# Half of the first layer's output turned by a DRAM trip and VectorE's square transposes, half by TensorE, with the three written-out orders replaced

## Chip, cores and metric

The kernel runs on one core of one Trainium2 chip, on real inputs, and is judged by the device time of that core in microseconds (us), lower being better. All arithmetic that matters is f32.

## What is computed

64 independent graphs of 256 nodes each pass through two attention layers; `x` is 64 x 256 x 512, `adj` 64 x 256 x 256.

```python
h = relu(layernorm(x))
# layer 0: two attention products in a row, mask = adj or self
xl = (h @ W1)            # 512 -> 4 heads x 256
z  = elu(concat_heads(softmax(mask(leaky_relu(a_src + a_dst))).T @ xl) + b1)   # 256 x 1024
xl = (z @ W2)            # 1024 -> 512, one head
x  = x + softmax(...).T @ xl + b2
# layer 1: eight heads of 64
h  = relu(layernorm(x))
xp = h @ W_proj          # 512 -> 512
x  = x + relu(softmax(mask(leaky_relu(...))) @ xp)
```

The change concerns `z`, the first attention's output: 256 nodes by 1024 features, the features of heads 0 and 1 in columns 0 to 511. It must be turned (features on partitions) before TensorE can multiply it with `W2`.

## The kernel before, in words

The program is one straight list of instructions, without loops on the chip. A `Graph` object has one method for each step of a graph's work, and three strings, `head`, `order` and `tail`, write out by hand the order in which the steps of neighbouring graphs are emitted: `0 gat1 1 0` in round `r` is step `gat1` with arguments 1, 0 of graph `r + 0`, and `-1 m3 p5` a step of graph `r - 1`. `head` runs once, `order` for r = 1 to 63, `tail` once. So three graphs are always in flight, and every engine works through its own instructions in the order of the strings: an instruction that waits holds up all that its engine has after it. SyncE (SP) issues nearly all DMAs and is such a queue too.

The steps that are named later, for one graph:

- `load`, `masks`, `stats1`, `norm1`: input, adjacency masks (VectorE), layer statistics (VectorE, then a power on GpSimd), normalisation (ScalarE, L189).
- `away1`, `turn1`: the normalised `h` is written to DRAM (`kept_h`, L203), read back with its 32-column squares on other partitions (L204), and turned by VectorE's 32 x 32 transposes (`back`, L209).
- `m1a`, `m1b`, `m2`, `m3`: the products with W1 (two halves), W2 and W_proj. Each is done with 7 block products, `p1` to `p7` (L54), over sums of the turned operand that `left` makes on GpSimd (L215 to L218). `p1` reads block 0 of the turned operand, `p2` block 1, `p5` block 3 (the first of GpSimd's sums), `p6` block 2 (the second). `p1`, `p6` and `p7` each copy their PSUM sum by ScalarE (`kept`, L60); `p2`, `p3` and `c22` add on VectorE (L260).
- `exp1`/`rows1`/`edges1`/`gat1`/`out1`/`elu1`: the first attention. `rows` sends the exponentials through DRAM to broadcast them (L239, L244), `edges1 h` makes the weights of head h (ScalarE L289, VectorE L290), `gat1 g t` is the product of heads 2g and 2g+1 for half t of the nodes (TensorE L394), `out1 g t` normalises (VectorE L402, L404) and makes exp(-relu(-z)) on ScalarE (L407, L408), `elu1 g t` ends it on VectorE (L413).
- `turn2 r k`: 4 of TensorE's transposes (L196) into a PSUM tile, and ScalarE's copy to the operand `h1s` of `m2` (L422). Four such steps turn the 16 blocks of `z`.
- `edges2`/`gat2`/`out2`, `stats3`/`norm3`/`turn3`, `edges3`/`gat3`/`out3`/`store`: second attention (TensorE L448, VectorE L455, L458), second normalisation, turned by TensorE with ScalarE's copy (L196, L229), third attention (L500, L506, L508) and output. `cap3` issues DMA transposes of the mask.

PSUM tiles `pm` have four buffers, `sum` two, the transposes' tiles `pt` two. `z` has one buffer for each half of the nodes, `h1s` one.

Of the kernel before, what the change touches and what calls it, by code (L numbers as in the profile page):

```python
# [17 lines left out]
P = 128  # L18
# [79 lines left out]
def short_path(ctx, tc, flags, x, adj, w1, att_src1, att_dst1, b1, w2, att_src2, att_dst2, b2, w_proj, w_att,  # L98
               b_att, out):

    nc = tc.nc
    B, N, D = x.shape
    H1, F1 = att_src1.shape
    HF = H1 * F1
# [23 lines left out]
    ident = const.tile([P, P], F32, name="ident")  # L128
# [21 lines left out]
    w2_sb = const.tile([P, 7, HC // 2, L2 + Q], F32, name="w2_sb")  # L150
# [42 lines left out]
    def turn(h, c, pt):  # L193
        for k in range(2):
            for t in range(T):
                nc.tensor.transpose(pt[:, k, t * P:(t + 1) * P], h(t, c + k), ident)  # L196
# [95 lines left out]
    class Graph:  # L292
# [120 lines left out]
            nc.vector.scalar_tensor_tensor(z, self.e["ez", g, t], -1.0, z, ALU.add, ALU.max)  # L413
# [12 lines left out]

        def exp2(self):
# [138 lines left out]
    class Weights:  # L566
# [49 lines left out]


    head = """
        0 turn0, w dots1 0, 0 masks, 0 m1b p1, w dots1 2, w dots1 5, w sums1 1, w dots1 1, 0 m1b p6, w dots1
        3, 0 bias, 0 m1b p2, 0 m1b p7, w dots2 0, 0 m1b p5, w dots1 4, w dots1 6, w dots1 7, 0 m1a p1, w  # L620
        sums1 0, 0 m1b c22, 0 m1b p4, 0 m1a p6, w dots2 3, 0 m1a p7, 0 m1a p5, w dots2 2, w dots2 7, w dots2
        5, 0 m1a p2, 0 m1a c22, w dots2 1, 0 m1a p3, w dots2 6, 0 m1a p4, w dots2 4, w columns2, 0 m1b p3, w
        sums2 0, w sums2 1, 0 exp1, 0 rows1, w sums2 2, 0 caps, w sums2 3, 0 edges1 1, 0 edges1 0, 0 edges1
        3, 0 cap3, 0 edges1 2, 0 gat1 0 0, 0 out1 0 0, 0 gat1 0 1, 0 out1 0 1, 0 gat1 1 0, 0 elu1 0 0, 0
        out1 1 0, 0 elu1 0 1, w load3, 0 gat1 1 1, 1 load, 0 out1 1 1, w dots3 7, 1 stats1, 0 turn2 0 0, 0
        elu1 1 0, 1 masks, 0 turn2 0 1, 0 elu1 1 1, 1 norm1, w dots3 1, 0 m2 p1, w dots3 2, w dots3 0, w
        dots3 6, 1 away1, 0 turn2 1 0, 0 turn2 1 1, w dots3 5, w dots3 4, w dots3 3, 1 turn1, 0 m2 p6, w
        sums3 0, 0 m2 p2, w sums3 1, w sums3 2, 0 m2 p7, 0 m2 p4, 0 m2 p5, 1 m1a p1, 1 m1a p6, 0 m2 c22, 1
        m1a p5, 0 m2 p3, 0 exp2, 0 rows2, 1 m1a p7, 1 m1a c22, 1 m1b p1, w sums3 3, 1 m1a p4, 1 m1a p3, 1
        m1a p2, 1 exp1, 1 rows1, 1 bias, 1 m1b p6, 1 m1b p2, 1 m1b p5, 1 caps  # L630
    """
# [13 lines left out]
    tail = """
        -2 range, 0 m1b p5, 0 m1a p2, -1 edges2, -2 gat3 0 0, 0 m1a c22, 0 m1b p6, -2 gat3 0 1, -2 out3 0 1,
        0 m1b p2, -2 edges3 5, -1 gat2 0, 0 exp1, 0 rows1, 0 m1a p4, -1 out2 0, -1 stats3 0, -2 edges3 7, -1
        gat2 1, -2 gat3 1 0, -1 out2 1, -1 stats3 1, -1 norm3, -2 out3 0 0, -2 gat3 1 1, -2 out3 1 1, -1
        turn3, -1 m3 p1, -1 m3 p2, -1 m3 p5, -1 m3 p6, -1 m3 p7, -1 m3 c22, -2 out3 1 0, -1 m3 p4, -1 m3 p3,
        -1 exp3, -1 rows3, -1 range, -1 edges3 1, -1 edges3 4, -1 edges3 0, -1 edges3 3, -1 edges3 2, -1  # L650
        edges3 5, -1 edges3 7, -1 edges3 6, -1 gat3 0 0, -1 gat3 0 1, -2 store, -1 gat3 1 1, -1 out3 0 1, -1
        out3 1 1, -1 gat3 1 0, -1 out3 0 0, -1 out3 1 0, -1 store
    """
# [295 lines left out]
```

## Time and profile before

| what | value |
|---|---|
| median of 3 runs | 3218.17 us (3216.63 to 3219.29) |
| profiled execution | 3218.9 us, its span 3217.2 us |
| granted TensorE clock, mean | 0.993 |
| TensorE (PE) busy | 3133.7 us, 97% of the span |
| weight loads (PEld) busy | 2670.7 us, 83% |
| VectorE (DVE) busy | 2282.5 us, 71% |
| ScalarE (ACT) busy | 1917.4 us, 60% |
| GpSimd (POOL) busy | 1179.1 us, 37% |
| SP's queue of DMAs | 31.9% of 16 DMA engines |

Times in the profile are microseconds unless marked ns. A line of groups gives the code line, engine, operation, output <- inputs, shape and count, then busy time and the mean ns of one instruction, then the engine's idle time before them and what ended it. A line of the timeline gives start, length, engine, line and count of merged instructions. Matmuls overlap each other, so the step from one start to the next, and not the length of one, is what a matmul costs the engine.

### The profile page before, as it was taken

How to read it: one execution, taken by the hardware profiler on the slowest of the kernel's cores; microseconds unless marked ns; L12 is line 12 of the kernel's file. 1: busy time of each engine (PE TensorE's matmuls, PEld its weight loads, DVE VectorE, ACT ScalarE, POOL GpSimd, SP SyncE). 2: the span in 40 equal slices, each digit the busy share in tenths (PEclk: the TensorE clock that was granted, in tenths of full speed). 3: DMA queues.
4: the chain of work that ended last, by engine and by line, in shares of the span. 5: the costliest groups of instructions: out<-in, count | busy, mean ns of one | idle time of the engine just before them, and what ended most of it. 6: DMA issues, size and time to landing. Idle time of an engine off the chain costs nothing. (4 is left out here: it accounts for less than half of the span.)

```text
span 3217.2 us, 60904 instructions
## 1 busy us (share of the span) xinstructions
PE 3133.7 (97%) x21808; PEld 2670.7 (83%) x21808; DVE 2282.5 (71%) x6379; ACT 1917.4 (60%) x4867; POOL 1179.1 (37%) x1434
## 2 busy tenths in 40 slices
PE   4999999999999999999999999999999999999997
PEld 3788888888888888888888888888888888888886
DVE  7667677677677677676676776776776776776765
ACT  2456566656666665665565566566666666655654
POOL 2343343333433433433433433434434334334332
PEclk8999999999999999999999999999999999999999
DMA  4233333333333333333333333332333333333331
GB/s 143 57 95 83 89 88 91 83 91 87 89 87 92 88 86 84 96 81 90 97 80 90 88 89 83 91 92 83 92 87 88 88 91 88 81 89 96 81 90 35
DMA packets 439842, 281.49 MB, mean 87 GB/s; under 512 B 109168, under 2 KB 389744, under 8 KB 439536
## 3 DMA queue, kind: packets, MB, share of 16 engines
q1 hardware_dynamic: 438160, 275.43, 31.9%
q8 instruction: 177, 2.90, 0.4%
q10 hardware_dynamic: 1376, 2.10, 0.2%
q14 instruction: 129, 1.06, 0.1%
HBM read 199.36 MB, written 69.70 MB: 84 GB/s over the span
## 5 line engine op out<-in xcount | busy, mean ns | idle before, releaser
L289 ACT ACTIVATE wy<-bc,exs_sb 128x256 f32<-128x256 f32 x1646 | 706.9, 498 | 176.1 <-DMA bc<-kept 129.3
L260 DVE TENSOR_TENSOR xl<-pm,kept 128x256 f32<-128x256 f32 (+2 forms) x768 | 321.5, 419 | 285.8 <-PE pm L54 208.7
L510 POOL TENSOR_TENSOR x<-x,o 128x256 f32<-128x256 f32 x256 | 181.1, 728 | 916.0 <-DVE r L506 884.4
L394 PE MATMUL pm<-xl,e 128*128 128x257 f32 x2048 | 489.9, 386 | 17.6 <-DVE e L290 13.6
L290 DVE SCALAR_TENSOR_TENSOR e<-wy,exs_sb,cap 128x256 f32<-128x256 f32 x1024 | 435.8, 478 | 92.4 <-ACT wy L289 92.4
L54 PE MATMUL sum<-w_sb,h1s 128*128 128x257 f32 x2048 | 489.0, 381 | 9.3 <-POOL h1s L216 7.0
L60 ACT ACTIVATE kept<-sum 128x264 f32<-128x264 f32 (+3 forms) x768 | 276.5, 376 | 341.9 <-PE sum L54 336.6
L54 PEld LDWEIGHTS sum<-w_sb,h1s 128*128 128x128 f32 x2048 | 389.3, 190 | 68.7 <-POOL h1s L216 7.2
L394 PEld LDWEIGHTS pm<-xl,e 128*128 128x128 f32 x2048 | 374.3, 190 | 84.0 <-DVE e L290 14.9
L54 PE MATMUL pm<-w_sb,h1s 128*128 128x257 f32 x1536 | 371.1, 383 | 10.4 <-DVE xl L260 6.5
L54 PEld LDWEIGHTS pm<-w_sb,h1s 128*128 128x128 f32 x1536 | 287.0, 190 | 74.9 <-POOL hs L216 20.1
L181 POOL TENSOR_TENSOR rstd<-ve,neg_half 128x2 f32<-128x2 f32 x128 | 117.6, 919 | 630.3 <-DVE ve L179 630.3
L500 PEld LDWEIGHTS pm<-xl,e 128*64 128x64 f32 x8192 | 251.0, 138 | 45.4 <-DVE e L290 23.4
L54 PE MATMUL sum<-w1a_sb,hs 128*128 128x260 f32 x1024 | 269.6, 386 | 11.7 <-ACT kept L60 4.5
L290 DVE SCALAR_TENSOR_TENSOR e<-wy,exs_sb,mask 128x256 f32<-128x256 f32 x640 | 270.3, 480 | 13.1 <-ACT wy L289 12.8
L54 PE MATMUL sum<-w1b_sb,hs 128*128 128x256 f32 x1024 | 271.9, 388 | 2.9 <-ACT hs L353 1.5
L500 PE MATMUL pm<-xl,e 128*64 128x65 f32 x8192 | 270.1, 224 | 2.1 <-DVE e L290 1.3
L54 PE MATMUL sum<-wp_sb,hs 128*128 128x264 f32 x1024 | 270.8, 387 | 1.3 <-ACT kept L60 1.1
L407 ACT ACTIVATE ez<-z 128x512 f32<-128x512 f32 x256 | 159.6, 623 | 178.5 <-DVE z L404 178.5
L404 DVE SCALAR_TENSOR_TENSOR z<-pm,r,b_sb 128x256 f32<-128x256 f32 x512 | 247.8, 484 | 18.3
L448 PE MATMUL pm<-xl,e 128*128 128x257 f32 (+1 forms) x1024 | 242.9, 380 | 1.1 <-DVE e L290 1.1
L54 PEld LDWEIGHTS sum<-w1a_sb,hs 128*128 128x128 f32 x1024 | 191.4, 190 | 50.2 <-issue 15.2
(99 smaller groups left out, 5013.4 us busy)
## 6 DMA issues: line engine op xcount, KB each, us to landing
bc<-kept SPq DMA_DIRECT2D x380, 256.0 KB, 5.7
xs<-in_x_dram SPq DMA_DIRECT2D x64, 512.0 KB, 3.9
out_dram<-x SPq DMA_DIRECT2D x64, 512.0 KB, 2.8
kept_h<-h SPq DMA_DIRECT2D x63, 512.0 KB, 3.2
h<-kept_h SPq DMA_DIRECT2D x63, 512.0 KB, 3.7
ad<-in_adj_dram SPq DMA_DIRECT2D x64, 256.0 KB, 4.3
bc<-kept SPq DMA_DIRECT2D x63, 128.0 KB, 4.8
kept<-wt SPq DMA_DIRECT2D x190, 16.0 KB, 1.4
```

The costliest lines, as they stand in the source:

```text
L54: self.nc.tensor.matmul(to[:, :self.n], self.lhs[:, i, c, :], self.rhs[:, i, c, :], start=(first and c == 0), stop=(last and c == self.nk ...
L60: self.nc.scalar.activation(s[:, :self.n], self.sum[:, :self.n], AF.Copy)
L181: nc.gpsimd.tensor_tensor(rstd, ve[:, 0, :], neg_half, ALU.pow)
L260: nc.vector.tensor_tensor(dst, pm, add, ALU.add)
L289: nc.scalar.activation(wy.rearrange("p (t j i) -> p t j i", t=T, j=4), bc, AF.Copy, scale=yw)
L290: nc.vector.scalar_tensor_tensor(dst, wy, xw, mask, ALU.max, op)
L394: nc.tensor.matmul(pm[:, :Q + 1], self.e[1, h][:, s, t * P:(t + 1) * P], xl1[:, s, h, L1:], start=(s == 0), stop=(s == T - 1))
L404: nc.vector.scalar_tensor_tensor(z[:, sl], pm[:, :Q], r, b1_sb[:, sl], ALU.mult, ALU.add)
L407: nc.scalar.activation(ez, z[:, 2 * g * F1:2 * (g + 1) * F1], AF.Relu, scale=-1.0)
L448: nc.tensor.matmul(pm[:, :n], self.e[2][:, s, t * P:(t + 1) * P], xl2[:, s, half, L2:L2 + n], start=(s == 0), stop=(s == T - 1))
L500: nc.tensor.matmul(pv[q:q + 64, h, :], self.e[3, a * G + h][:, s, t * P + q:t * P + q + 64], xl3[:, s, a * G + h, :], start=(s == 0), stop ...
L510: nc.gpsimd.tensor_tensor(to, to, o.rearrange("p h k -> p (h k)"), ALU.add)
```

## The change

Heads 0 and 1 of `z` (the first 512 columns) leave TensorE's transposes, for every graph but the first and the last. `send2 t`, after `elu1 0 t`, writes these columns of one half of the nodes to DRAM and reads them back into the same place with the 32-column squares redistributed; `back2 t` turns them by one transpose of VectorE straight into `h1s`. For the first and the last graph `back2` uses TensorE and ScalarE as before. `turn2 k` remains for heads 2 and 3. Since the new path leaves the features of heads 0 and 1 in another order, the first 512 rows of W2 are loaded in that order. The strings `head`, `order` and `tail` are written anew: `head` now reaches into round 2, `order` runs for r = 2 to 62, and `tail` takes more of the last rounds.

```diff
-        def turn2(self, r, k):
-            if r == 0 and k == 0:
+        def send2(self, t):
+            if t == 0:
                 self.a2 = work.tile([P, 7, HC // 2, P], F32, name="h1s", bufs=1)
                 self.m2 = Product(nc, ps_sum, ps_mm, work, self.a2, w2_sb, put2)
+            if 0 < self.b < B - 1:
+                z = self.zt[t][:, :HF // 2]
+                kept = dram.tile([4, P, P], F32, name="kept_z")
+                nc.sync.dma_start(kept.rearrange("a p e -> p a e"), z.rearrange("p (a e) -> p a e", a=4))
+                nc.sync.dma_start(z, kept.rearrange("a (j q) e -> (a j) (q e)", q=4))
+
+        def back2(self, t):
+            z, a = self.zt[t][:, :HF // 2], self.a2[:, 4 * t]
+            if 0 < self.b < B - 1:
+                nc.vector.transpose(a.rearrange("p k (j q) -> p q k j", q=4), z.rearrange("p (q i c) -> p q c i", q=4, c=4))
+            else:
+                pt = ps_tr.tile([P, 2, N], F32, name="pt")
+                for k in range(HC // 2):
+                    nc.tensor.transpose(pt[:, k // 2, k % 2 * P:(k % 2 + 1) * P], z.rearrange("p (m k) -> p k m", k=4)[:, k],
+                                        ident)
+                nc.scalar.activation(a.rearrange("p k q -> p (k q)"), pt.rearrange("p k q -> p (k q)"), AF.Copy)
+
+        def turn2(self, k):
             pt = ps_tr.tile([P, 2, N], F32, name="pt")
-            turn(lambda t, c: self.zt[t][:, c * P:(c + 1) * P], 4 * r + 2 * k, pt)
-            nc.scalar.activation(self.a2[:, r:r + 5:4, 2 * k:2 * k + 2], pt.rearrange("p k (t q) -> p t k q", t=T),
-                                 AF.Copy)
-            if r == 1 and k == 1:
+            turn(lambda t, c: self.zt[t][:, c * P:(c + 1) * P], 4 + 2 * k, pt)
+            nc.scalar.activation(self.a2[:, 1:6:4, 2 * k:2 * k + 2], pt.rearrange("p k (t q) -> p t k q", t=T), AF.Copy)
+            if k == 1:
                 left(self.a2, HC // 2)
...
-    bring(w2_sb, w2, 0, 0, (nc.sync, nc.sync))
+    for half in range(2):
+        nc.sync.dma_start(blocks(w2_sb)[0][half][:, :, -Q:],
+                          w2[:HF // 2, half * Q:(half + 1) * Q].rearrange("(p c) f -> p c f", p=P))
...
     order = """
-        -2 edges3 7, -2 gat3 0 0, -2 edges3 5, -2 gat3 0 1, -1 edges2, 0 m1b p7, -2 out3 0 1, -2 out3 0 0,
-        -1 gat2 0, 0 m1b c22, -1 out2 0, -1 stats3 0, 0 m1b p3, -1 gat2 1, 0 edges1 0, 0 edges1 1, 0 m1b p4,
-        -1 out2 1, 0 cap3, 1 load, 0 gat1 0 0, 0 edges1 2, 0 edges1 3, 0 out1 0 0, -2 gat3 1 1, -2 gat3 1 0,
-        -1 stats3 1, 0 gat1 0 1, -1 norm3, -2 out3 1 1, -2 out3 1 0, -2 store, 0 out1 0 1, 0 elu1 0 0, 0
-        elu1 0 1, 0 gat1 1 0, -1 turn3, 0 out1 1 0, 0 gat1 1 1, 0 out1 1 1, 1 stats1, -1 m3 p1, 0 turn2 0 0,
-        0 turn2 0 1, 0 elu1 1 1, 0 elu1 1 0, -1 m3 p2, -1 m3 p5, 1 masks, 1 norm1, -1 m3 p6, 0 m2 p1, 0
-        turn2 1 0, 0 turn2 1 1, 1 away1, -1 m3 p7, 1 bias, -1 m3 c22, 0 m2 p2, -1 m3 p4, -2 range, -1 m3 p3,
-        -1 exp3, -1 rows3, 1 turn1, 0 m2 p6, 0 m2 p5, 0 m2 p7, 1 caps, 1 m1a p1, 0 m2 c22, 0 m2 p3, 0 m2 p4,
-        0 exp2, 0 rows2, 1 m1a p6, -1 edges3 0, -1 edges3 1, 1 m1b p1, 1 m1a p7, 1 m1a p5, 1 m1a c22, -1
-        edges3 2, 1 m1a p2, -1 edges3 4, 1 m1a p3, -1 edges3 3, 1 m1a p4, 1 m1b p2, 1 exp1, 1 rows1, -1
-        edges3 6, 1 m1b p6, 1 m1b p5
+        0 m1b p3, -1 gat2 1, 0 gat1 0 0, -1 out2 1, 0 edges1 2, 0 edges1 3, 0 m1b p4, 0 out1 0 0, -2 gat3 1
+        1, -2 gat3 1 0, 0 gat1 0 1, 1 load, -1 stats3 1, -2 out3 1 1, 0 elu1 0 0, -1 norm3, 0 cap3, 0 out1 0
+        1, 0 gat1 1 0, 0 send2 0, 0 out1 1 0, 0 elu1 0 1, 0 send2 1, 0 gat1 1 1, -1 turn3, -1 m3 p1, 0 out1
+        1 1, 0 elu1 1 0, -2 out3 1 0, -1 m3 p5, -2 store, -1 m3 p6, 1 stats1, 0 elu1 1 1, 0 back2 0, -1 m3
+        p2, 1 norm1, 0 turn2 0, -1 m3 p7, 1 masks, 0 back2 1, 0 turn2 1, -1 m3 c22, 0 m2 p1, 0 m2 p2, -1 m3
+        p4, 1 away1, -1 m3 p3, 0 m2 p6, -1 exp3, 0 m2 p5, 1 caps, -1 rows3, 1 bias, 0 m2 p7, 1 turn1, 1 m1a
+        p1, 0 m2 c22, 0 m2 p4, 0 m2 p3, 0 exp2, -2 range, 0 rows2, 1 m1a p6, -1 edges3 0, 1 m1b p1, -1
+        edges3 1, 1 m1a p7, 1 m1a p5, 1 m1a c22, -1 edges3 4, 1 m1a p2, -1 edges3 2, 1 m1a p3, -1 edges3 3,
+        1 m1a p4, 1 exp1, 1 rows1, -1 edges3 6, 1 m1b p6, -1 edges3 7, -1 gat3 0 0, -1 edges3 5, -1 gat3 0
+        1, 1 m1b p2, 0 edges2, 1 m1b p7, 1 m1b p5, -1 out3 0 0, -1 out3 0 1, 0 gat2 0, 1 m1b c22, 0 out2 0,
+        0 stats3 0, 1 edges1 0, 1 edges1 1
     """
...
-    for r in range(1, B):
+    for r in range(2, B - 1):
         run(order, r)
```

More of the change, by code (lines that the diff above doesn't have):

```diff
@@ L618, in short_path @@
     head = """
[L619 to L628, printed above, removed]
@@ L629, in short_path @@
-        m1a p5, 0 m2 p3, 0 exp2, 0 rows2, 1 m1a p7, 1 m1a c22, 1 m1b p1, w sums3 3, 1 m1a p4, 1 m1a p3, 1
-        m1a p2, 1 exp1, 1 rows1, 1 bias, 1 m1b p6, 1 m1b p2, 1 m1b p5, 1 caps
+        0 turn0, w dots1 0, 0 masks, 0 m1b p1, w dots1 2, w dots1 5, w sums1 1, w dots1 1, 0 m1b p2, 0 m1b
+        p6, 0 m1b p7, w dots2 0, w dots1 3, 0 m1b p5, w dots1 4, 0 m1b c22, w dots1 6, w dots1 7, 0 m1b p4,
+        0 m1a p1, w sums1 0, 0 m1a p6, w dots2 3, 0 m1a p7, w dots2 2, w dots2 7, w dots2 5, 0 m1a p5, 0
@@ new lines, in short_path @@
+        bias, 0 m1a p2, w dots2 1, 0 m1a c22, 0 m1a p3, 0 m1a p4, w dots2 4, w dots2 6, w columns2, 0 m1b
+        p3, w sums2 0, w sums2 1, 0 exp1, 0 rows1, w sums2 2, 0 caps, w sums2 3, 0 edges1 1, 0 edges1 0, 0
+        edges1 3, 0 edges1 2, 0 gat1 0 0, 0 cap3, 0 out1 0 0, 0 gat1 0 1, 0 out1 0 1, 0 gat1 1 0, 0 elu1 0
+        0, 0 send2 0, 0 out1 1 0, w load3, 0 elu1 0 1, 0 send2 1, 0 gat1 1 1, 1 load, 0 back2 0, 0 out1 1 1,
+        0 back2 1, w dots3 7, 1 stats1, 0 elu1 1 0, 1 masks, 0 elu1 1 1, 1 norm1, w dots3 1, 0 m2 p1, w
@@ new lines, in short_path @@
+        dots3 2, w dots3 0, w dots3 6, 1 away1, 0 turn2 0, 0 turn2 1, w dots3 5, 0 m2 p6, w dots3 4, w dots3
+        3, 1 turn1, w sums3 0, w sums3 1, 0 m2 p2, w sums3 2, 0 m2 p7, 0 m2 p5, 1 m1a p1, 0 m2 p4, 1 m1a p6,
+        0 m2 c22, 0 m2 p3, 1 m1a p7, 1 m1a p5, 0 exp2, 0 rows2, 1 m1a c22, 1 m1b p1, 1 m1a p4, w sums3 3, 1
+        m1a p3, 1 m1a p2, 1 bias, 1 exp1, 1 rows1, 1 m1b p6, 1 m1b p2, 1 caps, 1 m1b p5, 0 edges2, 1 m1b p7,
+        0 gat2 0, 1 m1b c22, 0 out2 0, 0 stats3 0, 1 edges1 0, 1 m1b p3, 0 gat2 1, 1 edges1 1, 1 m1b p4, 0
@@ new lines, in short_path @@
+        out2 1, 1 edges1 2, 1 gat1 0 0, 1 edges1 3, 1 out1 0 0, 0 stats3 1, 2 load, 1 gat1 0 1, 0 norm3, 1
+        elu1 0 0, 1 cap3, 1 out1 0 1, 1 elu1 0 1, 1 send2 0, 1 send2 1, 1 gat1 1 0, 0 turn3, 1 out1 1 0, 1
+        gat1 1 1, 1 out1 1 1, 2 stats1, 0 m3 p1, 0 m3 p2, 1 elu1 1 0, 1 elu1 1 1, 2 norm1, 0 m3 p6, 0 m3 p5,
+        1 turn2 0, 1 back2 0, 1 m2 p1, 1 back2 1, 0 m3 p7, 2 away1, 2 bias, 2 masks, 1 turn2 1, 0 m3 c22, 1
+        m2 p2, 0 m3 p4, 0 m3 p3, 0 exp3, 0 rows3, 2 turn1, 1 m2 p6, 1 m2 p5, 1 m2 p7, 2 m1a p1, 1 m2 c22, 1
@@ L631, in short_path @@
+        m2 p3, 2 m1a p6, 1 m2 p4, 1 exp2, 1 rows2, 0 edges3 1, 2 m1a p5, 2 m1a p7, 2 m1a c22, 0 edges3 2, 0
+        edges3 4, 2 m1b p1, 2 m1a p3, 0 edges3 3, 2 m1a p2, 0 edges3 6, 0 edges3 0, 2 m1b p6, 2 m1a p4, 2
+        m1b p2, 2 exp1, 2 rows1, 0 edges3 5, 0 gat3 0 1, 0 gat3 0 0, 0 edges3 7, 2 m1b p5, 1 edges2, 2 m1b
+        p7, 0 out3 0 0, 1 gat2 0, 2 caps, 0 out3 0 1, 2 m1b c22, 1 out2 0, 1 stats3 0, 2 edges1 0, 2 edges1
+        1
     """
     order = """
-        -2 edges3 7, -2 gat3 0 0, -2 edges3 5, -2 gat3 0 1, -1 edges2, 0 m1b p7, -2 out3 0 1, -2 out3 0 0,
@@ L644, in short_path @@
+        p1, 0 m2 c22, 0 m2 p4, 0 m2 p3, 0 exp2, -2 range, 0 rows2, 1 m1a p6, -1 edges3 0, 1 m1b p1, -1
[3 more added lines that the diff above has]
+        0 stats3 0, 1 edges1 0, 1 edges1 1
     """
     tail = """
-        -2 range, 0 m1b p5, 0 m1a p2, -1 edges2, -2 gat3 0 0, 0 m1a c22, 0 m1b p6, -2 gat3 0 1, -2 out3 0 1,
@@ L647, in short_path @@
[L647 to L651, printed above, removed]
@@ L652, in short_path @@
-        out3 1 1, -1 gat3 1 0, -1 out3 0 0, -1 out3 1 0, -1 store
+        -1 m1b p3, -1 edges1 2, -2 gat2 1, -1 cap3, -2 out2 1, -1 m1b p4, -1 edges1 3, -1 gat1 0 0, -1 out1
+        0 0, -3 gat3 1 1, -3 out3 1 1, -2 stats3 1, -3 gat3 1 0, -1 gat1 0 1, -2 norm3, -3 out3 1 0, -1 out1
+        0 1, -3 store, -1 elu1 0 0, -1 elu1 0 1, -1 send2 0, -1 gat1 1 0, -1 send2 1, -2 turn3, -1 out1 1 0,
+        -1 gat1 1 1, -1 out1 1 1, -2 m3 p1, -1 elu1 1 1, -1 elu1 1 0, -2 m3 p2, -1 back2 0, -2 m3 p5, -2 m3
@@ new lines, in short_path @@
+        p6, -1 back2 1, -1 turn2 0, -1 m2 p1, -1 turn2 1, -2 m3 p7, -2 m3 c22, -1 m2 p2, -2 m3 p4, -3 range,
+        -2 m3 p3, -2 exp3, -1 m2 p6, -2 rows3, -1 m2 p5, -1 m2 p7, -1 m2 c22, -1 m2 p3, -2 edges3 0, -2
+        edges3 3, -1 m2 p4, -1 exp2, -1 rows2, -2 edges3 1, -2 edges3 2, -2 edges3 4, 0 exp1, 0 m1b p5, -2
+        edges3 6, -2 gat3 0 0, 0 m1b p2, -2 range, -1 edges2, -2 gat3 0 1, 0 m1a p2, -2 edges3 5, 0 m1b p6,
+        -1 gat2 0, -2 out3 0 1, 0 rows1, -1 out2 0, -1 stats3 0, -1 gat2 1, 0 m1a c22, -2 edges3 7, -2 gat3
@@ L653, in short_path @@
+        1 0, -1 out2 1, -1 stats3 1, -1 norm3, -2 out3 0 0, -2 gat3 1 1, -1 turn3, -1 m3 p1, 0 m1a p4, -1 m3
+        p2, -1 m3 p5, -1 m3 p6, -1 m3 p7, -2 out3 1 1, -1 m3 c22, -2 out3 1 0, -1 m3 p4, -1 m3 p3, -1 exp3,
+        -1 rows3, -1 range, -1 edges3 4, -1 edges3 1, -1 edges3 0, -2 store, -1 edges3 3, -1 edges3 2, -1
+        edges3 6, -1 gat3 0 1, -1 gat3 0 0, -1 edges3 5, -1 edges3 7, -1 out3 0 1, -1 gat3 1 1, -1 out3 1 1,
+        -1 gat3 1 0, -1 out3 0 0, -1 out3 1 0, -1 store
     """
```

## The prediction

> **What bounds the kernel now.** I read the page's busy shares first, then the windows, then the timeline of one round.
>
> ```profile
> PE 3133.7 (97%) x21808; PEld 2670.7 (83%) x21808; DVE 2282.5 (71%) x6379; ACT 1917.4 (60%) x4867; POOL 1179.1 (37%) x1434
> ```
>
> ```profile
> 100.00:800.00 700.00, 692.06 (x4801) 590.55 (x4801) 497.98 (x1379) 426.28 (x1088) 253.31 (x307) 1.00 0.33 87
> 800.00:1600.00 800.00, 796.80 (x5570) 681.93 (x5567) 573.72 (x1598) 491.45 (x1244) 303.03 (x367) 1.00 0.33 89
> ```
>
> The window columns are the stretch, its length, then the busy time of PE, PEld, DVE, ACT and POOL. In the middle PE is busy for 796.8 of 800 us; its idle time lies in the first 100 us (46 us) and the last 117 (17 us). So the middle is bound by PE, and what counts is the length of a round. Stores start at 363.58, 412.15 and 460.72 us: an undisturbed round takes **48.57 us**. PE's timeline then shows the transposes at issue:
>
> ```profile
> 1538.36 1.04 PE L196 MATMUL pt<-ident,z 128*128 128x128 f32 x8
> 1539.24 1.95 PE L54 MATMUL pm<-wp_sb,hs 128*128 128x264 f32 x8
> ...
> 1543.65 1.03 PE L196 MATMUL pt<-ident,z 128*128 128x128 f32 x8
> 1544.52 1.06 PE L54 MATMUL sum<-wp_sb,hs 128*128 128x264 f32 x4
> ```
>
> From start to start, 8 transposes hold PE for 0.88 us, and the eight at 1538.36 are those that go. DVE's timeline in the same round shows how near DVE is behind:
>
> ```profile
> 1523.50 1.08 DVE L458 SCALAR_TENSOR_TENSOR x<-pm,r,xs 128x256 f32<-128x256 f32 x2
> 1524.62 0.69 DVE L173 BATCH_NORM_STATS2 stats<-x 128x6 f32<-128x512 f32 x1
> ...
> 1539.06 0.68 DVE L173 BATCH_NORM_STATS2 stats<-xs 128x6 f32<-128x512 f32 x1
> ...
> 1540.94 1.28 DVE L413 SCALAR_TENSOR_TENSOR z<-ez,z 128x512 f32<-128x512 f32 x2
> ```
>
> DVE works almost without a pause from the end of `gat2 0` (PE, 1523.90) to the last `elu1` (1542.2), 18.3 us with 0.85 of idling, and the transposes of heads 2 and 3 follow on PE at 1543.65. In this stretch DVE is full although it has 71% over the whole, and it has 1.4 us to spare.
>
> **What the Trainium skill says.** "VectorE: DVE Perf Modes", section on the three transpose paths: VectorE turns 32 x 32 blocks only and lands in SBUF, TensorE turns a whole block and lands in PSUM. The trace agrees: `back` (L209) writes `hs` directly, 1134 ns each, where `turn2` needs ScalarE's copy of 594 ns (L422) after PE. "DMA: Bandwidth & Descriptors", Two DMAs through the same engine are not ordered: a read of what another DMA wrote must wait for its completion semaphore. SP's waits show it: 204.5 us in 63 waits of L204 for `kept_h`, 3.2 us each. "Perfetto Trace Analysis", Identifying the Most-Contended Engine: matmul busy time overstates how near PE is to its limit. Here PE is 97% busy and its weight loads 83%, so I count starts, not lengths.
>
> **The change, part by part.** It acts on 62 graphs.
>
> 1. PE: 8 transposes go, 0.88 us a graph, 54.6 us in all. The other bound is the groups' 132.8 us / 1024 = 130 ns each, 64 us, which counts overlaps. I take 54.6.
> 2. ACT: two copies of 594 ns go, 1.2 us a graph, on an engine at 60%: no time by themselves.
> 3. DVE: two transposes come. `back` has 136.0 us / 126 = 1.08 each, so 2.16 us a graph, 134 us in all; DVE goes to about 76%. They stand after the last `elu1`, where DVE is freer. If their cover goes, `m2 p1` waits for them.
> 4. SP: four DMAs of 256 KB a graph. Issue is 0.37 each, 1.5 us a graph. Landing lies between 1.4 us (16 KB) and 3.2 (512 KB write) or 3.7 (512 KB read); I take 2.4 and 2.8, about 5.3 for the trip. By the order `load` and `cap3` stand ahead of `send2 0`; then come both trips, `store`, `away1`, `rows3`. SP now waits for L239's and L203's inputs 560.9 and 594.7 us in all, so it has room. I work out (below) that `send2 1` starts 13 us after the end of `gat2 0`, lands at about 18.5 and is wanted by `back2 1` at about 20: 1.5 us of slack, cost nothing. DMA load rises by 65 of 281 MB.
> 5. W2's loading in another row order: same bytes, the same two DMAs. Nothing, in the first 45 us behind VectorE's weight work.
> 6. The new order, which decides. I follow one round from the end of `gat2 0` to `turn2 0`.
>
> *DVE's side*, steps from start to start: `out2 0` ends 0.67 after `gat2 0`. Then `stats3 0` 0.82, `edges1 0` and `1` 1.59, the sum of `m1b p3` 0.31, `out2 1` 1.03, `edges1 2` and `3` 1.59, `out1 0 0` 1.19, `stats3 1` 1.09, an `out3` 0.55, `elu1` 0.64, `out1 0 1` and `1 0` 2.38, `elu1` 0.64, `out1 1 1` 1.19, `elu1` 0.64, `out3` 0.55, `stats1` 1.88, `elu1 1 1` 0.64: 17.4 us. `norm3` (1.5 us of ACT) now stands ahead of an `ez` pair (1.27), which makes one `elu1` about 0.25 late: **17.65**.
>
> *PE's side*: `m1b p3` 0.86, `gat2 1` 1.73, four `gat1` 7.0, `m1b p4` 0.87, two `gat3` 2.1, `turn3` 0.91, `m3 p1`, `p5`, `p6`, `p2` 3.56: 17.1 us of work. Before, the same stretch was 19.75; the eight transposes and `m2 p1` have left it. But new waits appear. `m3 p1` now follows `turn3` directly, where `gat1 1 1` (1.73) lay between them. The end of the trace before has this neighbourhood: transposes from 3187.34, the copy at 3187.92 for 0.59 a tile, `m3 p1` at 3188.57. Four transposes (0.44), 0.25 to ACT, 0.6 of copy make 1.3 against the 0.91 that `turn3` lasts: 0.4 of waiting. `m3 p5` needs GpSimd's first sum (731 ns) after the second copy: 1.85 + 0.08 + 0.75 = 2.7 after `turn3`'s start, against 1.3 + 0.9: another 0.5. `gat1`'s PSUM tiles wait for DVE's `m1b p3` sum and `out1 0 1`, about 0.15 each. Sum 1.2, bounded by 0 and 1.8. So PE reaches `turn2 0` after 17.1 + 1.2 = **18.3**, later than DVE's 17.65.
>
> *The rest of the round*: before 48.57 - 19.75 = 28.82; plus `m2 p1` 1.74; less about 0.35 that PE waited for `m2 p3` (its tile waits for `c22`, and `m2 p4` now lies between; in the trace `m1a p1` there takes 1.19 for 0.88). That is 30.2. `rows2` to `gat2 0` keeps its 11.8 us, and `edges2` now comes just 0.2 ahead of need.
>
> Round: 18.3 + 30.2 = 48.5 (48.4 to 48.5), against 48.57. Of 0.88 + 0.35 us won, some 1.1 goes to the new waits. I take 0.15 us a round, 62 x 0.15 = 9 us. Head and tail have 63 us of idling, in dependency chains that stay (weights, first DMA, last graph): bounds of 8 gained to 5 lost, I take 5 gained. Against the profiled execution's own 3218.9 us (its span of 3217.2 and 1.7 around it) this gives 3205; that execution is 0.7 above the median, so **3204**.
>
> **The rivals.** What a measurement of this kernel tells from no change is about 0.2%, 6.4 us.
>
> *A, PE's new waits are hidden:* DVE's 17.65 is the bound of the stretch, or its floor of 17.4. The round is 17.4 + 30.2 = 47.6, a gain of 1.0 x 62 = 60 with 4 of the head: about 3155 to 3170. For it: the trace has a PE that waits for nearly nothing in the middle, and GpSimd's 37%. Against it: `turn3` without cover, measured above.
>
> *B, slower: ACT becomes late behind `turn3`.* ACT's list there is `norm3`, `ez` of `out1 0 1`, `ez` of `1 0`, `turn3`'s copies, `kept`, `ez` of `1 1`, all in order. If the copies come half a us later than I think, `m3 p1`, `p5` and the last `elu1` are later by as much. The break-even is a stretch of 18.4 us; at 18.8 the round is 49.0 and the kernel gains nothing but loses 62 x 0.43 = 27: 3240 with 5 for the ends uncertain. For it: DVE and ACT have no slack left in this stretch, where before 1.4 us absorbed a late DMA (two rounds near 500 us took 49.2 and 49.5). Against it: ACT has lost 1.2 us a graph.
>
> *C, the DRAM trip is late.* Were it over 6.8 us instead of 5.3, DVE would stand at `back2 1`, with `m3`'s sums behind it; another 1 us costs PE little, since `m2 p6` has 2 us over. Up to 3225. 512 KB now takes 3.2 + 3.7 = 6.9, so 256 KB is unlikely to.
>
> *D, nothing measurable:* the gain and the waits cancel, 3212 to 3224.
>
> **How the numbers follow.** Partial gain (my forecast, 3180 to 3211) 0.41; A 0.16; B with C's worse half 0.27; D 0.16. Faster by over 0.2%: 0.57; within: 0.16; slower: 0.27. The range from 3168 to 3238 leaves out A's far end and B's.
>
> **What the changed profile would show.** Right: rounds of 48.4 us between stores; PE waits of L54 for ACT `hs` L229 and POOL `hs` L215 once a round, which the trace before hardly has; 124 new DVE transposes at 1.1 us; L196 on `z` falling from 1024 to 512; no DVE wait of weight for the read of `kept_z`. Wrong: rounds of 47.6 without these waits (A), or PE waiting at `turn2` for DVE's `z` L413 (B), or DVE's new transposes waiting for a DMA (C). A head or tail that moves by over 8 us would break the sum too.

## The result and the profile after

| what | before | after |
|---|---|---|
| median, four runs each on the same chip | 3217.55 us | **3254.7 us** (3252.35 to 3256.69) |
| ratio of the times | | 1.0115, interval 1.0097 to 1.0132 |
| span of the profiled execution | 3217.2 us | 3250.9 us |
| granted TensorE clock, mean | 0.993 | 0.992 |
| undisturbed round, store to store (median) | 48.58 us | 49.04 us |
| all rounds of the middle, mean | 48.80 us | 49.30 us |

The kernel became slower by 1.15%. The busy line of the page and one window of the middle (stretch, length, then busy time and count of PE, PEld, DVE, ACT and POOL, clock, DMA share, GB/s) say where to look:

```profile
PE 3121.5 (96%) x21312; PEld 2614.4 (80%) x21312; DVE 2471.1 (76%) x6503; ACT 1877.7 (58%) x4743; POOL 1189.3 (37%) x1434
```

```profile
800.00:1600.00 800.00, 783.99 (x5380) 658.11 (x5381) 617.89 (x1614) 473.16 (x1198) 295.00 (x354) 1.00 0.39 108
```

PE has lost its 496 transposes, but it now idles for 16.0 of 800 us in the middle where it idled for 3.2. In 800 us there are about 16.3 rounds, so that is some 0.8 us a round of new waiting. Most of the loss is in the rounds. Counted on PE from the start of `gat2 0` of graph 2 to that of graph 62, the 60 rounds take 28.9 of the 33.7 us by which the span grew. Up to the first of these marks 4.2 us are lost, in the first two rounds (52.4 and 51.6 us from one `gat2 0` to the next, where before took 49.5 and 48.6), and 0.7 behind the last.

PE's timeline of one round shows the place. `gat2 0` ended at 1446.63 (the start of PE's next product), and the stretch that the prediction followed runs from there to the first transpose of `z`:

```profile
1459.55 1.04 PE L196 MATMUL pt<-ident,h 128*128 128x128 f32 x8
1460.84 1.16 PE L54 MATMUL sum<-wp_sb,hs 128*128 128x264 f32 x4 [0.25 <-ACT hs L229]
1462.13 1.16 PE L54 MATMUL pm<-wp_sb,hs 128*128 128x264 f32 x4
...
1464.91 0.27 PE L196 MATMUL pt<-ident,z 128*128 128x128 f32 x1
1465.55 0.55 PE L196 MATMUL pt<-ident,z 128*128 128x128 f32 x3 [0.37 <-DVE z L413]
```

The lines are `turn3`, `m3 p1`, `m3 p5`, and `turn2 0` in two pieces. PE arrives at `turn2 0` at 1464.91, which is 18.28 us after `gat2 0`. The first transpose there uses a half of `z` that is ready. The second needs the other half, and starts at 1465.55. A transpose takes 0.11 from start to start, so without the wait it would have started at 1465.02: 0.53 us are lost. Now the same moment on DVE and POOL (L430 is the transpose of `back2`):

```profile
1463.54 0.73 POOL L218 TENSOR_TENSOR hs<-hs 128x256 f32<-128x256 f32 x1
1463.63 0.66 DVE L178 TENSOR_SCALAR ve<-mv 128x2 f32<-128x2 f32 x1
...
1464.20 0.15 DVE L179 TENSOR_SCALAR ve<-mv 128x2 f32<-128x2 f32 x1
...
1464.22 0.73 POOL L528 TENSOR_TENSOR x<-x,o 128x256 f32<-128x256 f32 x1
1464.27 1.23 DVE L413 SCALAR_TENSOR_TENSOR z<-ez,z 128x512 f32<-128x512 f32 x1
...
1465.42 1.12 DVE L430 STREAM_TRANSPOSE h1s<-z 128x512 f32<-128x512 f32 x1
```

L413 is the last `elu1`, on which PE waits. It starts 0.05 after GpSimd's addition of `out3 1 0` (L528) and takes 1.23 instead of 0.68 us. Just before, L178, an operation on two elements a partition, starts 0.09 after GpSimd's last partial sum of `hs` (L218) and takes 0.66 instead of 0.17. No wait is written beside either: the profile books the added time as **busy time of DVE**. The views of these two source lines give smallest, median and longest duration in ns, first of before, then of after:

```profile
L413 DVE SCALAR_TENSOR_TENSOR z<-ez,z x256: 681/687/716, 63.8 to 3152.3; 128x512 f32<-128x512 f32 x128
L178 DVE TENSOR_SCALAR ve<-mv x128: 168/170/172, 8.2 to 3184.5; 128x2 f32<-128x2 f32 x128
```

```profile
L413 DVE SCALAR_TENSOR_TENSOR z<-ez,z x256: 679/684/1230, 64.1 to 3185.8; 128x512 f32<-128x512 f32 x128
L178 DVE TENSOR_SCALAR ve<-mv x128: 168/170/666, 8.2 to 3216.2; 128x2 f32<-128x2 f32 x128
```

In before no instance is long; in after one of four `elu1` and one of two L178 is, in 61 rounds, so the medians stay. The long ones end where GpSimd's instruction lets them: L413 0.55 us after the end of L528, L178 0.02 after that of L218, in the median. Together they cost DVE 0.55 + 0.49 = 1.04 us a round. The views of waits of PE and of its weight loads (total, times, longest) show what follows from it, and the two waits behind `turn3`:

```profile
PE pt L196 <- DVE z L413: 24.8, 63, 1.0
PE sum L54 <- ACT hs L229: 15.3, 61, 0.3
```

```profile
PEld pm L54 <- POOL hs L215: 33.5, 61, 0.6
```

The Trainium skill has the mechanism, in "SBUF — State Buffer", Who interferes with whom: VectorE and GpSimd share one pair of ports as an exclusive lock. A VectorE instruction with both inputs in SBUF contends with a GpSimd instruction that reads SBUF, a `tensor_scalar` may in its two-port modes, and "Issue order, not op shape, decides who blocks." This agrees with the trace: L413 has two SBUF inputs and L178 is a `tensor_scalar`, and each started after GpSimd's instruction. Whether L178 ran in a two-port mode, no run here shows. That this and not the trip is the cause had to be tried.

### The profile page after: what moved, and what is told of

The parts are those of the page before. It is cut to its first block, busy times and chain, and to the rows that moved or that the text cites. A ratio compares the mean times of both kernels' runs of the same rounds, so it can differ in the third digit from the quotient of the medians.

```text
span 3250.9 us, 60717 instructions
## 1 busy us (share of the span) xinstructions
PE 3121.5 (96%) x21312; PEld 2614.4 (80%) x21312; DVE 2471.1 (76%) x6503; ACT 1877.7 (58%) x4743; POOL 1189.3 (37%) x1434
## 3 DMA queue, kind: packets, MB, share of 16 engines
q14 instruction: 133, 1.09, 0.1%
## 5 line engine op out<-in xcount | busy, mean ns | idle before, releaser
L394 PE MATMUL pm<-xl,e 128*128 128x257 f32 x2048 | 497.0, 391 | 25.5 <-DVE e L290 18.9
L60 ACT ACTIVATE kept<-sum 128x264 f32<-128x264 f32 (+3 forms) x768 | 293.8, 383 | 384.4 <-PE sum L54 378.4
L290 DVE SCALAR_TENSOR_TENSOR e<-wy,exs_sb,cap 128x256 f32<-128x256 f32 x1024 | 443.2, 480 | 82.5 <-ACT wy L289 82.4
L528 POOL TENSOR_TENSOR x<-x,o 128x256 f32<-128x256 f32 x256 | 183.6, 728 | 832.2 <-DVE r L524 661.8
L181 POOL TENSOR_TENSOR rstd<-ve,neg_half 128x2 f32<-128x2 f32 x128 | 117.8, 920 | 555.4 <-DVE ve L179 555.4
L54 PE MATMUL sum<-wp_sb,hs 128*128 128x264 f32 x1024 | 277.6, 394 | 17.0 <-ACT hs L229 15.3
L54 PE MATMUL sum<-w1b_sb,hs 128*128 128x256 f32 x1024 | 264.8, 381 | 2.1 <-ACT hs L353 1.6
L404 DVE SCALAR_TENSOR_TENSOR z<-pm,r,b_sb 128x256 f32<-128x256 f32 x512 | 247.7, 484 | 18.2
L54 PEld LDWEIGHTS sum<-wp_sb,hs 128*128 128x128 f32 x1024 | 184.4, 190 | 58.4 <-ACT hs L229 30.0
```

Source lines behind the costliest of these rows:

```text
L54: self.nc.tensor.matmul(to[:, :self.n], self.lhs[:, i, c, :], self.rhs[:, i, c, :], start=(first and c == 0), stop=(last and c == self.nk ...
L60: self.nc.scalar.activation(s[:, :self.n], self.sum[:, :self.n], AF.Copy)
L181: nc.gpsimd.tensor_tensor(rstd, ve[:, 0, :], neg_half, ALU.pow)
L290: nc.vector.scalar_tensor_tensor(dst, wy, xw, mask, ALU.max, op)
L394: nc.tensor.matmul(pm[:, :Q + 1], self.e[1, h][:, s, t * P:(t + 1) * P], xl1[:, s, h, L1:], start=(s == 0), stop=(s == T - 1))
L404: nc.vector.scalar_tensor_tensor(z[:, sl], pm[:, :Q], r, b1_sb[:, sl], ALU.mult, ALU.add)
```

## The experiments

Theory 1: GpSimd holds up L178 and the last `elu1`. Theory 2: `turn3`, which has lost its cover, and the waits for ScalarE's copy and GpSimd's sum behind it make PE late. Theory 3: the trip through DRAM (its DMAs, `back2`'s place) is at fault. All ratios are to the kernel before on the same chip.

**e1, GpSimd's addition later.** `out3` is split: with a last argument of 0 it leaves out GpSimd's addition, and the new step `add3` makes it. The addition of `out3 1 0` (L528, here L534) and the store go behind `norm1`; DVE's list of instructions does not change.

```diff
-        0 elu1 1 0, -2 out3 1 0, -1 m3 p5, -2 store, -1 m3 p6, 1 stats1, 0 elu1 1 1, 0 back2 0, -1 m3 p2,
-        1 norm1, 0 turn2 0
+        0 elu1 1 0, -2 out3 1 0 0, -1 m3 p5, -1 m3 p6, 1 stats1, 0 elu1 1 1, 0 back2 0, -1 m3 p2,
+        1 norm1, -2 add3 1 0, -2 store, 0 turn2 0
```

> The changed kernel, with one step of `order` split: of `out3 1 0` the VectorE part stays where it is, and only GpSimd's addition (L528) and the store behind it move to after `norm1`. VectorE's list of instructions is unchanged. Theory 1 (GpSimd's addition holds up the last `elu1`, which needs two SBUF operands): L413's long cases (1.23 us) go back to 0.68, the last `elu1` ends 0.55 earlier, PE's own arrival at `turn2 0` (18.3 us after `gat2 0`) takes over, rounds of 48.5 instead of 49.04 us, about 3222 us. Theory 2 (VectorE's list is simply too long, the long L413 is something else) and theory 3 (the DRAM trip's DMAs are at fault): no change, 3250 to 3259 us.

Measured: **3215.49 us**, ratio 1.0002 (0.9993 to 1.0010). By the two ratios that is some 36 of the 37 us that after loses, for moving one instruction of GpSimd that no other engine's compute waits for, and the store behind it. The source line of `elu1`, the timeline of DVE and POOL, and PE's `turn2 0` in e1:

```profile
L413 DVE SCALAR_TENSOR_TENSOR z<-ez,z x256: 676/681/694, 65.5 to 3147.9; 128x512 f32<-128x512 f32 x128
```

```profile
1445.18 0.73 POOL L218 TENSOR_TENSOR hs<-hs 128x256 f32<-128x256 f32 x1
1445.29 0.66 DVE L178 TENSOR_SCALAR ve<-mv 128x2 f32<-128x2 f32 x1
1445.93 0.68 DVE L413 SCALAR_TENSOR_TENSOR z<-ez,z 128x512 f32<-128x512 f32 x1
...
1447.39 0.73 POOL L534 TENSOR_TENSOR x<-x,o 128x256 f32<-128x256 f32 x1
```

```profile
1446.56 0.65 PE L196 MATMUL pt<-ident,z 128*128 128x128 f32 x4
```

L413 is back at 0.68, while L178 is still held up, as it must be since L218 has not moved. PE no longer waits at `turn2 0`, and the round is 48.50 us. This is the round that the prediction gave (48.4 to 48.5). So theory 1 is shown for nearly all of the loss: GpSimd's addition at that place makes `elu1` late, and PE with it. The store moved as well, but e7 shows that an instruction of GpSimd alone lengthens an `elu1`.

**e2, no trip.** After's three orders, but `back2` uses TensorE and ScalarE for every graph and `send2` sends nothing.

```diff
-            if 0 < self.b < B - 1:
+            if False:
```

> The changed kernel with its new orders, but heads 0 and 1 of all graphs turned by TensorE and ScalarE (no `kept_z` DMAs, no added VectorE transposes). Theory 1 (the round waits for the last `elu1` of VectorE, the trip costs nothing): four transposes before `turn2 0` fill most of PE's wait there, four after it cost 0.44 us: rounds of about 49.5, some 3281 us. Theory 3 (the trip's DMAs or transposes are at fault): faster than the changed kernel, 3220 us or less.

Measured: 3356.88 us, ratio 1.0442 (1.0424 to 1.0459), a round of 50.82. Theory 3 falls: taking the trip away costs some 105 us more. And the long `elu1` stays without it, though PE doesn't come for it at that moment here:

```profile
L413 DVE SCALAR_TENSOR_TENSOR z<-ez,z x256: 679/684/1230, 65.9 to 3292.4; 128x512 f32<-128x512 f32 x128
```

The size was missed. The transposes' 0.88 a round explain half of the 1.78 by which the round grew. On top comes a wait of `turn2 1` for ScalarE's copy, which sets it back by 1.28, while the 0.53 lost at `turn2 0` are gone. PE's timeline (L441 is the copy of a `turn2`):

```profile
1459.87 0.66 PE L196 MATMUL pt<-ident,z 128*128 128x128 f32 x4 [1.09 <-ACT h1s L441]
```

There are two PSUM tiles `pt`, and in this order the copy of `turn2 0` that frees one stands behind `norm1` on ScalarE, which in that round waited 1.21 us for GpSimd's part of the statistics (L183). The trip thus takes two copies, and the two tiles that they hold, out of a place where ScalarE is late, which my "no time by themselves" had not seen.

**e3, the trip in the old orders.** Before's three strings, with `send2` and `back2` put in, two of the four `turn2` taken out and `m2 p1` moved behind `turn2` and `m3 p7` (the cut shows a part of `order`).

```diff
-        0 elu1 0 0, 0 elu1 0 1, 0 gat1 1 0 ... 0 turn2 0 0, 0 turn2 0 1, 0 elu1 1 1, 0 elu1 1 0, -1 m3 p2
+        0 elu1 0 0, 0 send2 0, 0 elu1 0 1, 0 send2 1, 0 gat1 1 0 ... 0 elu1 1 1, 0 elu1 1 0, 0 back2 0, 0 back2 1, -1 m3 p2
...
-        -1 m3 p6, 0 m2 p1, 0 turn2 1 0, 0 turn2 1 1, 1 away1, -1 m3 p7
+        -1 m3 p6, 0 turn2 0, 0 turn2 1, 1 away1, -1 m3 p7, 0 m2 p1
```

> The three orders of the kernel before, with the trip put in: `send2` after each `elu1` of heads 0 and 1, `back2 0` and `back2 1` after the last two `elu1`, the eight transposes gone, and `m2 p1` moved behind `turn2 1` and `m3 p7`, since its operand now comes later. Theory 1 in its wider form (the stretch up to the last `elu1` is as long as VectorE's work, 18.3 us, so that work taken from PE in it is not won): the transposes wait for `z`, rounds of 48.9 us, about 3236 us. Rival (only the new orders are at fault, the trip alone wins its 0.88 us a graph): rounds of 47.7, 3164 us.

Measured: 3342.16 us, ratio 1.0401 (1.0383 to 1.0418); slower, as expected, but by 128 us where some 20 were expected. PE has three kinds of waits that are rare in the kernel before (there 6.1 us in 15 times, 0.6 in one, 6.7 in 38). The view of waits, and the first two kinds in the timeline of one round:

```profile
PE sum L54 <- ACT kept L60: 101.1, 131, 1.0
PE pt L196 <- DVE z L413: 22.2, 63, 0.6
PE pm L54 <- DVE xl L260: 22.1, 54, 1.7
```

```profile
1495.37 1.13 PE L54 MATMUL sum<-wp_sb,hs 128*128 128x264 f32 x4 [0.59 <-ACT kept L60]
1496.85 1.06 PE L196 MATMUL pt<-ident,z 128*128 128x128 f32 x8 [0.35 <-DVE z L413]
1498.90 1.13 PE L54 MATMUL sum<-wp_sb,hs 128*128 128x264 f32 x4 [0.99 <-ACT kept L60]
```

They are `m3 p6`, `turn2`, and `m3 p7`: 1.9 us together, in every round. The third kind, for DVE's additions, is over 0.6 us only eleven times. The eight transposes and `m2 p1` had stood among `m3`'s products and covered its copies; without them these are bare. No `elu1` is held up by GpSimd here; the longest takes 715 ns. So the new order is no ornament. Of the two orders tried with the trip so far, it is the one that makes the trip bearable.

**e4, another order.** After's string `order` with `turn3` two steps earlier, `stats1` ahead of the last two `elu1`, `m3 p7` ahead of `turn2 0`, and `out3 1 0` with its addition behind `turn2 1`, its store behind `away1` (not in the cut).

```diff
-        0 send2 0, 0 out1 1 0, 0 elu1 0 1, 0 send2 1, 0 gat1 1 1, -1 turn3, -1 m3 p1, 0 out1
-        1 1, 0 elu1 1 0, -2 out3 1 0, -1 m3 p5, -2 store, -1 m3 p6, 1 stats1, 0 elu1 1 1, 0 back2 0, -1 m3
-        p2, 1 norm1, 0 turn2 0, -1 m3 p7, 1 masks, 0 back2 1, 0 turn2 1, -1 m3 c22
+        0 send2 0, -1 turn3, 0 out1 1 0, 0 elu1 0 1, 0 send2 1, 0 gat1 1 1, -1 m3 p1, 0 out1
+        1 1, 1 stats1, -1 m3 p5, -1 m3 p6, 0 elu1 1 0, 0 elu1 1 1, 0 back2 0, -1 m3 p2, -1 m3
+        p7, 1 norm1, 0 turn2 0, 1 masks, 0 back2 1, 0 turn2 1, -2 out3 1 0, -1 m3 c22
```

> The changed kernel with `order` alone changed in this stretch: `turn3` goes ahead of `gat1 1 1`, so that ScalarE's copies and GpSimd's sums for `m3` have a cover and are over before the last two `elu1`; `stats1` ahead of these; `m3 p7` ahead of `turn2 0`; `out3 1 0` behind `turn2 1` and its store behind `away1`. Theory 1: no lengthened L178 and L413, the last `elu1` ends 17.9 us after `gat2 0`, PE has 17.4 + 0.9 us of other work by then and no waits for `hs`: rounds of 47.6 to 48.0, 3167 to 3191 us. Theory 2 (only VectorE's count matters): the moved `out3` takes 0.55 off the list, 3220 us. Theory 3: about 3250 us.

Measured: **3177.26 us**, ratio 0.9882 (0.9864 to 0.9900), inside what was expected. PE's timeline of the stretch in e4, with no wait left in it (from `turn3` over `m3 p1`, `p5`, `p6`, `p2`, `p7` to `turn2`):

```profile
1474.26 1.04 PE L196 MATMUL pt<-ident,h 128*128 128x128 f32 x8
...
1476.87 1.05 PE L54 MATMUL sum<-wp_sb,hs 128*128 128x264 f32 x4
...
1480.43 1.05 PE L54 MATMUL sum<-wp_sb,hs 128*128 128x264 f32 x4
1481.32 1.04 PE L196 MATMUL pt<-ident,z 128*128 128x128 f32 x8
```

`gat2 0` ended at 1463.06, so the stretch is 18.26 us and now holds `m3 p7` (0.89) as well. The shortest rounds, about a third of them, take 47.56 (the median of all is 47.79), which is the number of rival A. No L413 is over 694 ns and no L178 over 172.

**e5, `turn3` alone.** After with only e4's move of `turn3`.

```diff
-        0 send2 0, 0 out1 1 0, 0 elu1 0 1, 0 send2 1, 0 gat1 1 1, -1 turn3, -1 m3 p1
+        0 send2 0, -1 turn3, 0 out1 1 0, 0 elu1 0 1, 0 send2 1, 0 gat1 1 1, -1 m3 p1
```

> The changed kernel with one move in `order`: `turn3` ahead of `gat1 1 1` and of `out1 1 0`. It covers ScalarE's copies and GpSimd's first sum for `m3`, so the two waits of `m3 p1` and `m3 p5` (0.9 us on PE in the changed kernel) go; but GpSimd's sums come earlier too and meet the `elu1` before last, and `out3`'s addition still meets the last one. If the last `elu1` of VectorE is what the round waits for, little is won: it ends 18.4 to 18.9 us after `gat2 0`, rounds of 48.6 to 49.0, 3228 to 3253 us. If PE's uncovered `turn3` was the loss: rounds of 48.1, about 3198 us.

Measured: 3225.88 us, ratio 1.0038 (1.0023 to 1.0052), a round of 48.64. If PE's bare `turn3` had been the loss, 3198 was due, and it isn't. PE's waits for `hs` do go, yet PE gains nothing from arriving earlier; it stands at `turn2 0` for DVE longer than before:

```profile
1450.94 0.27 PE L196 MATMUL pt<-ident,z 128*128 128x128 f32 x1
1452.09 0.55 PE L196 MATMUL pt<-ident,z 128*128 128x128 f32 x3 [0.88 <-DVE z L413]
```

So theory 2 falls too. e5 is a little faster than after, and with `hs` ready earlier GpSimd's sums and L528 run earlier: L178 is at most 171 ns and L413 at most 827. Yet the last `elu1` ends only 0.4 sooner, 18.47 us after `gat2 0` in the median of the rounds where after has 18.88, though some 0.9 of blocking is gone. `turn3` now sets `gat1 1 1` back, and DVE, which needs that product, comes 0.5 later to the `elu1` before last. A new delay of DVE took the place of half of the old one.

**e6, `m3 p7` put back.** e4 with `m3 p7` behind `turn2 0`, as in after.

```diff
-        0 back2 0, -1 m3 p2, -1 m3 p7, 1 norm1, 0 turn2 0, 1 masks
+        0 back2 0, -1 m3 p2, 1 norm1, 0 turn2 0, -1 m3 p7, 1 masks
```

> The reordered kernel e4 with `m3 p7` put back behind `turn2 0`. PE then reaches `turn2 0` 17.4 us after `gat2 0`, the last `elu1` ends at 17.8: it waits 0.4 us a round, 25 us in all, 3202 us against 3177 for e4. If the order of these two doesn't matter: 3177 us.

Measured: 3195.84 us, ratio 0.9940 (0.9923 to 0.9956), 18.6 us more than e4. One block product of 0.89 us ahead of `turn2 0` is worth 0.3 to 0.4 us a round: it fills the time until DVE has `z`. Without it PE waits there for L413 again, 13.7 us in 63 waits. The medians over the rounds, counted from the end of `gat2 0`, show which side is late:

| run | last `elu1` ends | PE is at `turn2 0` |
|---|---|---|
| after | 18.88 us | 18.28 us |
| e1 | 18.33 us | 18.29 us |
| e5 | 18.47 us | 17.37 us |
| e6 | 17.85 us | 17.44 us |
| e4 | 17.85 us | 18.33 us |

Only in e4 does PE come clearly later than DVE.

**e9, `m1b p3` earlier.** e4 with `m1b p3` ahead of `edges1 0` and `1` in all three strings (the cut shows `order`).

```diff
-        0 m1b p3, -1 gat2 1, 0 gat1 0 0
+        -1 gat2 1, 0 gat1 0 0
...
-        0 stats3 0, 1 edges1 0, 1 edges1 1
+        0 stats3 0, 1 m1b p3, 1 edges1 0, 1 edges1 1
```

> The reordered kernel e4 with `m1b p3` emitted ahead of `edges1 0` and `1` in all three orders, so that VectorE's sum, which frees the PSUM tile that the second product of `gat1 0 0` takes, is not queued behind them (weight loads of L394 wait 34 us for it in e4). If that tile is what the product waits for: 0.2 us a round, some 3165 us. Rival: `edges1 1` itself comes late by as much (0.3 us of VectorE's work moved ahead of it), no change, 3177 us.

Measured: **3168.54 us**, ratio 0.9856 (0.9840 to 0.9873), the lowest ratio here, though its interval still touches that of e4. The shortest rounds stay at 47.56; the mean of the rounds falls from 48.05 to 47.90, 9 us in 62 rounds and all that it gains on e4. PE's 29 waits of `gat1` for this sum in e4 (10.2 us) are gone.

**e7 and e8, the lock by itself.** To e4, behind `out3 1 1` and so beside the first two `elu1`: in e7 four GpSimd multiplications that read SBUF, in e8 sixteen GpSimd memsets that only write it. Their results are used by nothing else, apart from `b2` (`b_sb` in the view), which e7 multiplies by ones. The cut shows e7; e8 has `nc.gpsimd.memset(idle, 1.0)` sixteen times in its place, `idle` being a tile of 128 x 96.

```diff
+        def pool(self):
+            for _ in range(4):
+                nc.gpsimd.tensor_tensor(b2_sb[:, :Q], b2_sb[:, :Q], ones.to_broadcast([P, Q]), ALU.mult)
...
+        -2 out3 1 1, 0 pool, 0 elu1 0 0
```

> The reordered kernel e4 with four more GpSimd multiplications a round (128 x 256, in place on b2 by ones, which leaves b2 as it is), emitted after `out3 1 1`, so that GpSimd is busy with SBUF operands when VectorE comes to the second `elu1` of heads 0 and 1. Theory 1: that `elu1` (one of four L413) starts no later but takes until GpSimd's chain leaves it room, 1.2 us or more instead of 0.68, in nearly every round; the time goes up by 10 to 40 us. Theory 2: L413 stays at 0.68.

> As the kernel with four more GpSimd multiplications, but with sixteen GpSimd memsets of 128 x 96 in their place, which read nothing from SBUF and keep GpSimd busy for about as long. Theory 1 in the narrow form (only a GpSimd instruction that reads SBUF holds up VectorE): L413 at 0.68 throughout, time as e4, about 3177 us. Wide form (any busy GpSimd does): L413 lengthened as there.

Measured: e7 3178.81 us, ratio 0.9891 (0.9862 to 0.9920); e8 3198.41 us, ratio 0.9945 (0.9923 to 0.9967). The times went the other way round from what was expected, so first the durations. The timelines of e7 and of e8, DVE and POOL, at the second `elu1` (e8 has one line more ahead of it, so `elu1` is L414 there):

```profile
1425.58 2.69 POOL L419 TENSOR_TENSOR b_sb<-b_sb,ones 128x256 f32<-128x256 f32 x4
...
1427.70 1.11 DVE L413 SCALAR_TENSOR_TENSOR z<-ez,z 128x512 f32<-128x512 f32 x1 [0.25 <-ACT ez L408]
```

```profile
1437.98 3.72 POOL L420 MEMSET idle<- 128x96 f32 x16
...
1440.13 0.69 DVE L414 SCALAR_TENSOR_TENSOR z<-ez,z 128x512 f32<-128x512 f32 x1 [0.25 <-ACT ez L409]
```

Under multiplications `elu1` takes 1.11, in 60 rounds, under memsets 0.69, and in all of e8 no `elu1` takes over 694 ns. For an instruction with two SBUF inputs this is what the section of the skill says: a GpSimd instruction that reads SBUF blocks it, one that only writes doesn't. L404, which reads one operand from PSUM, ran three times a round beside e7's multiplications and never took over 488 ns. What was measured is narrower than the section's words, though: in 61 rounds of e4 an `elu1` starts while GpSimd's power (L181, which reads two elements a partition) has 0.64 us left, and takes its usual 0.68.

So the mechanism is seen by itself, but my price for it was wrong: e7's 0.43 us a round cost nothing measurable. At that place nobody waits for DVE soon: from the start of this `elu1` to the statistics behind the next `out1` it is 2.28 us in both runs, since in e8 DVE waits for PE's `gat1 1 1` instead. An `elu1` is dear only where PE comes for `z` next. Why e8 is some 20 us slower than e4 I can only half say. The memsets last 3.7 us where the multiplications last 2.7, so the partial sums of `hs` end some 0.5 later and L218 holds up L178 again (up to 483 ns), and PE takes 0.17 us longer from `m3 p1` to `m3 p4` in the median. Another 0.18 in the mean lies between the first `gat3` and `turn3`, where `gat1 0 0` waits more often for the sum of `m1b p3` (41 times instead of 29); for that I have no cause.

## Why the prediction was wrong

Predicted were 3204, measured 3254.7, outside the range of 3168 to 3238. Of the 51 us between them the rounds make 38 (9 to be won, 29 lost) and the ends 10. Step by step:

- **PE's side was right.** Predicted 18.3 from `gat2 0` to `turn2 0`, with waits for ScalarE's copy and GpSimd's sum of 1.2; PE arrived after 18.28, with these waits in the two views above. (The products listed add up to 17.0, not 17.1, which changes nothing.)
- **The rest of the round was right.** Predicted 30.2; from `turn2 0`'s second transpose, set back by the one ahead of it (1465.44 on that count), it is 49.04 - 18.81 = 30.2.
- **DVE's side failed: the term 17.65.** Each row in it was a duration from before, where no GpSimd instruction ran beside L178, and where GpSimd's addition had only 0.16 us left when an `elu1` began. I moved these two, and moved GpSimd's instructions with `out3` and `m3`, and kept the durations: what GpSimd does to DVE was put at nothing. In after the last `elu1` ends 18.87 after `gat2 0`: 17.83 of the list, 0.18 over my sum, and 1.04 of blocking. DVE passed PE, and the stretch went from PE's 18.3 to DVE's 18.8.
- **The break-even of rival B, 18.4, and its price for 18.8** (27 us lost in the rounds, 29 measured) were nearly right, and so was its sign, PE waiting at `turn2` for L413. They hold for any delay of that size; the cause that it named was wrong. ScalarE was not late: its `ez` for the last `elu1` ended 0.67 us before that started.
- **The trip was right.** Write and read land in 2.5 and 2.7 us (estimated 2.4 and 2.8), as the lines of DMA issues show, and DVE's `back2` never waits for them:

```profile
kept_z<-z SPq DMA_DIRECT2D x124, 256.0 KB, 2.5
z<-kept_z SPq DMA_DIRECT2D x124, 256.0 KB, 2.7
```

- **ACT's copies "no time by themselves" was not right** in the new order: e2 shows that a wait for them would cost about 1 us a round there. It does not enter the sum of after, but it belongs to what the trip is worth.
- **The ends failed too, by 10 us**: they were to gain 5 and lost 5 (4.2 up to `gat2 0` of graph 2, 0.7 at the end). This is a second mistake. With `elu1` freed, e1 has the predicted round and its 60 rounds take 7.9 us less than before's, about as predicted (9 in 62), but its ends lose 4.9 as well, and so it only equals the kernel before. Why the first two rounds are long stays open.

The warning was in the profile before, and I passed over it. The group of `exp2`'s addition on 16 elements a partition, before and, for comparison, in e4:

```profile
L476 DVE TENSOR_TENSOR lg<-lg,batt_sb 128x16 f32<-128x16 f32 x64 | 72.8, 1137 | 0.0
```

```profile
L494 DVE TENSOR_TENSOR lg<-lg,batt_sb 128x16 f32<-128x16 f32 x64 | 11.9, 186 | 0.0
```

An addition of 16 elements that takes 1137 ns is not slow arithmetic. In before it starts 0.14 us after one of GpSimd's sums of `h1s` (128 x 512, 1.27 us) and ends 0.03 us after it: it is a blocked instruction. In e4 it starts when such a sum has 0.11 us left, and takes 186.

## What to carry to other kernels

When an order is changed, a DVE duration may be carried over only together with what GpSimd does beside it: look for rows whose time does not fit their size, and for every DVE instruction with two SBUF inputs on the path (here also for a `tensor_scalar`, L178) ask which GpSimd instruction will be running when it starts. Where PE comes for its result at once, keep GpSimd's long reads away from it; elsewhere the same blocking can cost nothing, as in e7. And taking work off the busiest engine takes away cover: the order must be found again around what then stands bare, here worth some 83 us between after and e9 with the same work.

## What the hardware showed that I had not expected

- A blocked DVE instruction is booked as busy until GpSimd's has ended, and then needs most of its own time if it is long: L178 on 2 elements goes from 0.17 to 0.66 us and ends 0.02 after GpSimd's, an addition on 16 elements goes from 0.17 to 1.16 and ends 0.03 after, an `elu1` goes from 0.68 to 1.23 and ends 0.55 after.
- It works the other way round too: GpSimd's power (L181) takes 1.14 us instead of 0.70 in the 62 or 63 times in each run that it starts during an `elu1`, and in e5 one of GpSimd's sums of `hs` takes 1.18 instead of 0.73 where it starts during one.
- In after's timeline L173's statistics of one input, 0.66 us, ran beside GpSimd's sums at their usual length, as did L430's transposes beside GpSimd's power: not every DVE instruction is held up.
- Four transposes and their copy can cost more by the copy's place on ScalarE (1.09 us of waiting in e2) than by TensorE's own 0.44, where PSUM tiles are short.
